# First 64 queries of every diagonal chunk: half of TensorE's columns for scores, half of its rows for values, two heads side by side

## The chip, the cores and the metric

One NeuronCore of one Trainium2 chip. The core has five engines with queues of their own, each strictly in the order written for it: TensorE (PE; its weight loads are listed separately as PEld), VectorE (DVE), ScalarE (ACT), GpSimd (POOL) and SyncE (SP, which issues DMAs). The metric is the device time of one execution in microseconds, as a median over several runs; less is better. Everything is float32.

## The reference

A transformer block on 4 batches of 512 tokens, 512 features: a layer norm, then causal attention and a mixture of experts on the same normed input, both added to the input.

```
xn  = layernorm(x)
c_Q = xn @ W_DQ.T ; c_KV = xn @ W_DKV.T                 # latents of 128
q = [c_Q @ W_UQ.T , rope(c_Q @ W_QR.T)]                 # 16 heads, 128 + 64
k = [c_KV @ W_UK.T , rope(xn @ W_KR.T)] ; v = c_KV @ W_UV.T
s = clip(q k^T, -80, 80), -inf where key > query
attn = softmax(s / sqrt(192)) @ v ; att = attn @ W_O.T
moe = shared_expert(xn) + sum over the 3 best of 7 experts, weighted
out = x + att + moe
```

The change concerns `s` and `softmax(s) @ v`. The kernel works in the latent: a head's query is folded with its key weights, so the keys of all heads are the latent `c_KV` itself (plus 64 rotary dimensions), and the values are again `c_KV`; each head's value and output weights are folded into one matrix that is applied afterwards.

## The kernel before

**Stages.** First the norm, the routing and the shared expert, then the routed experts (with the projections of attention woven in), and from about 663 us to the end attention alone. Attention is a loop over 32 pairs of heads (`pairs`: 4 batches of 8 pairs), counter `i`. All work of the loop is wrapped in `keep(...)`, so each engine's queue has the order in which the code is written.

**Layout.** `lat(b, n)` is a 128 x 512 slice of `xnT` for batch `b`: n=0 the query latent, n=1 the keys (latent on partitions, the 512 keys along the free axis), n=2 the rotary keys, twice, on partitions 0-63 for a pair's first head and on 64-127 for its second, n=3 the values (keys on partitions, in four chunks `kc` of 128). Scores are made transposed: keys on the 128 partitions, queries along the free axis. For key chunk `kc` only the queries from `kc*128` on count, so the chunks are 512, 384, 256 and 128 queries wide (`PT_W`). On the diagonal 128 x 128 block of each chunk the half above the diagonal is set to zero afterwards by a product with the triangle `tri` on GpSimd (L1445).

**One turn of the loop (L1658-1688), in TensorE's order.** `scores(i)`: eight matmuls of the latent part (L1408; heads j=0,1, chunks in the order 0, 2, 1, 3), then eight of the rotary part (L1419), where the two heads use rows 0-63 and 64-127 of the array and run side by side. Then for the next pair: `rotary_query` (L1260, output `pqr`), first `query` (L1275, `pq`); in even turns `sums` (L1508, the softmax denominators of two earlier pairs); `values(i-1, 0)` (L1489, `av`); the second `query`; `values(i-1, 1)`; in even turns from i=4 on `project_out` (L228 with tile `op`, 56 passes). A float32 matmul stands in the trace as two passes, each with a weight load of its own.

**PSUM.** Eight banks. Five have fixed names: `a0`, `a1` (chunk 0 of the two heads), `b0`, `b1` (chunks 1 and 3), `c` (chunk 2 of the first head). Three more, tag `pj`, go round: chunk 2 of the second head (`sd`), `pqr`, `pq`, `av`, `pq`, `av` take them one after the other, each waiting until the tile that had the bank has been read.

**After the scores (`weights`, L1429).** VectorE clips each bank into the SBUF tile `pt` (L1437), in the order a0, a1, sd, c, b0, b1; ScalarE takes the exponential in place (L1441), GpSimd masks. Between the third exponential and the fourth ScalarE copies `pqr` out (L1266, `qraw`); after the fifth it copies `pq`. VectorE then turns the rotary query (`rope`: L1246 and four times L1249; in odd turns right after the clips, in even turns after the reciprocal L1510 of the sums). GpSimd adds up the weights of a pair (`su`, L1469 and L1473). In odd turns VectorE ends with `divide` (L1540, L1546, L1549: four products and four sums over 128 x 512).

**Queues.** DMAs of the loop are SyncE's (`m`, `rb`) and GpSimd's (three row gathers `yg`, L1635, in even turns).

Of the kernel before, what the change touches and what calls it, by code (L numbers as in the profile page):

```python
# [12 lines left out]
I32 = mybir.dt.int32  # L13
# [23 lines left out]
QK_SCALE = 1.0 / math.sqrt(DH + DHR)  # L37

PT_W = [S - kc * P for kc in range(TPB)]


@with_exitstack
def kernel(
# [52 lines left out]
    for j in range(4):  # L96
# [11 lines left out]

    pos_i = const.tile([P, NTT, TOPK], I32, tag="pos_i", name="pos_i")
    wk = const.tile([P, NTT, TOPK], F32, tag="wk", name="wk")  # L110

    idx_i = const.tile([P, 4, NBLK], I32, tag="idx_i", name="idx_i")
    es_i = const.tile([P, NUNIT], I32, tag="es_i", name="es_i")

    used_i = const.tile([P, 1], I32, tag="used_i", name="used_i")
# [9 lines left out]
        [wb.tile([P, 2, D // 2], F32, tag=f"f{i}_{k}", name=f"f{i}_{k}") for k in range(3)]  # L125
        for i in range(3)
    ]

    half = [slice(0, S // 2), slice(S // 2, S)]

# [1062 lines left out]
    def project(b, psum):  # L1193

        if b % 2 == 0:
            two = psum(f"pj_kr_{b}")
            for c in range(DC):
                for j in range(2):
                    r = slice(j * DHR, (j + 1) * DHR)
                    keep(  # L1200
                        nc.tensor.matmul(
                            two[r, :],
                            krT[:, c, r],
                            xnT[:, c, ts(b + j, S)],
                            start=(c == 0),
                            stop=(c == DC - 1),
                        )
                    )
            raw = hw.tile([P, S], F32, tag="raw", name=f"kraw_{b}")
            keep(nc.scalar.copy(raw, two))  # L1210
            turned[b] = hw.tile([P, S], F32, tag="kr", name=f"kr_{b}", bufs=1)
            rope(turned[b], raw, f"k{b}")
        ps = []
        for wT, name in ((dqT, "cq"), (dkvT, "ckv")):
            p = psum(f"pj_{name}_{b}")
            for c in range(DC):
                keep(
                    nc.tensor.matmul(
                        p, wT[:, c, :], xnT[:, c, ts(b, S)], start=(c == 0), stop=(c == DC - 1)
                    )  # L1220
                )
            ps.append(p)
        keep(nc.scalar.copy(lat(b, 0), ps[0]))
        keep(nc.vector.tensor_copy(lat(b, 1), ps[1]))

        src = turned[b - b % 2][(b % 2) * DHR : (b % 2 + 1) * DHR, :]
        for j in range(2):
            keep(nc.vector.tensor_copy(lat(b, 2)[j * DHR : (j + 1) * DHR, :], src))

    turned = {}  # L1230

    def turn_keys(b, psum=None):
        if psum is None:
# [86 lines left out]
    def attention_steps(s):  # L1320

        for k in loads.get(s, []):
            loaded[k] = pieces[k][0]()
        for k in firsts.get(s, []):
            steps.extend(pieces[k][1](loaded[k]))
        if s == late + 2:
            dst, src = (lat(0, i).rearrange("p (k f) -> p k f", k=TPB) for i in (3, 1))
            steps.extend(turn4(dst, src))

    QUARTER = {0: 0, 4: 1, 7: 2, 10: 3}  # L1330
    POPS = (3, 2, 2, 2, 3, 3, 3, 3, 3, 3, 2, 1, 0, 0, 0, 0, 2, 2, 0, 0, 2)
# [45 lines left out]
    ap = ctx.enter_context(tc.tile_pool(name="ap", bufs=2))  # L1377
    mw = ctx.enter_context(tc.tile_pool(name="mw", bufs=1))
    ps_s = ctx.enter_context(tc.tile_pool(name="ps_s", bufs=1, space=PSUM))
    ps_p = ctx.enter_context(tc.tile_pool(name="ps_p", bufs=3, space=PSUM))  # L1380

    def psum(name):
# [7 lines left out]
    def scores(i):  # L1390
        b = pairs[i][0]
        qr, *qc = qs.pop(i)
        bank = {}
        for j in range(2):
            bank[j, 0] = ps_s.tile([P, S], F32, tag=f"a{j}", name=f"sa_{i}_{j}")
            bank[j, 1] = bank[j, 3] = ps_s.tile([P, S], F32, tag=f"b{j}", name=f"sb_{i}_{j}")
        bank[0, 2] = ps_s.tile([P, S], F32, tag="c", name=f"sc_{i}")
        bank[1, 2] = psum(f"sd_{i}")

        def where(j, kc):  # L1400
            o = 3 * P if kc == 3 else 0
            return bank[j, kc][:, o : o + PT_W[kc]]

        order = [(j, kc) for kc in (0, 2, 1, 3) for j in range(2)]
        for j, kc in order:

            keep(
                nc.tensor.matmul(  # L1408
                    where(j, kc),
                    lat(b, 1)[:, ts(kc, P)],  # L1410
                    qc[j][:, kc * P :],
                    start=(kc != 3),
                    stop=False,
                )
            )
        for j, kc in order:
            r = slice(j * DHR, (j + 1) * DHR)
            keep(
                nc.tensor.matmul(  # L1419
                    where(j, kc),  # L1420
                    lat(b, 2)[r, ts(kc, P)],
                    qr[r, kc * P :],
                    start=False,
                    stop=(kc != 1),
                )
            )
        return bank

    def weights(i, bank, then, behind):  # L1429

        pt = ap.tile([P, 5 * S], F32, tag="pt", name=f"pt_{i}")

        def clip(to, src):
            keep(nc.vector.tensor_scalar(to, src, CLIP, -CLIP, ALU.min, ALU.max))  # L1437

        def exp(t):

            keep(nc.scalar.activation(t, t, AF.Exp, scale=QK_SCALE))  # L1441

        def mask(t, at, k=1, step=P):
            m = t[:, at : at + P]
            keep(nc.gpsimd.tensor_mul(m, m, tri))  # L1445

        for j in range(2):
            a = pt[:, ts(j, S)]
            clip(a, bank[j, 0])
            exp(a)  # L1450
            mask(pt, PT[j, 0])
        half = 2 * P
        for j in (1, 0):
            clip(pt[:, PT[j, 2] : PT[j, 2] + half], bank[j, 2][:, :half])
        exp(pt[:, ts(2, S)])
        for j in range(2):
            mask(pt, PT[j, 2])
        then()
        for j in range(2):
            t = pt[:, ts(3 + j, S)]  # L1460
            clip(t, bank[j, 1])
            exp(t)
            mask(pt, PT[j, 1])
            mask(pt, PT[j, 3])
        behind()
        su = []
        for j in range(2):
            t = ap.tile([P, S], F32, tag="su", name=f"su_{i}_{j}", bufs=4)
            keep(nc.gpsimd.tensor_copy(t[:, :P], pt[:, PT[j, 0] : PT[j, 0] + P]))  # L1469
            for kc in range(1, TPB):  # L1470
                prev = pt[:, PT[j, 0] + P : PT[j, 0] + S] if kc == 1 else t[:, kc * P :]
                keep(
                    nc.gpsimd.tensor_add(  # L1473
                        t[:, kc * P :], prev, pt[:, PT[j, kc] : PT[j, kc] + PT_W[kc]]
                    )
                )
            su.append(t)
        pts[i], sus[i] = pt, su

    og = {}  # L1480

    def values(i, j):

        b, q = pairs[i][0], i // 2
        pt = pts[i]
        av = psum(f"av_{i}_{j}")
        for kc in range(TPB):
            keep(
                nc.tensor.matmul(  # L1489
                    av[:, kc * P :],  # L1490
                    lat(b, 3)[:, ts(kc, P)],
                    pt[:, PT[j, kc] : PT[j, kc] + PT_W[kc]],
                    start=(kc == 0),
                    stop=(kc == TPB - 1),
                )
            )
        if q not in og:
            og[q] = ap.tile([P, 4, S], F32, tag="og", name=f"og_{q}")
        keep(nc.scalar.copy(og[q][:, 2 * (i % 2) + j, :], av))
# [158 lines left out]
    for i in range(n):  # L1658
        more = i + 1 < n
        even = i % 2 == 0  # L1660
        q = i // 2 - 1
        held = scores(i)
        raw_copy, turn_q = rotary_query(i + 1, psum(f"pqr_{i + 1}")) if more else (nothing, nothing)
        qc_copy = query(i + 1, 0, psum(f"pq_{i + 1}_0")) if more else nothing
        weights(i, held, raw_copy, nothing if even else turn_q)
        qc_copy()
        if even and i > 0:
            spread_by_dma(q, sums(q))
        if even:
            turn_q()  # L1670
        if i > 0:
            values(i - 1, 0)
        if more:
            query(i + 1, 1, psum(f"pq_{i + 1}_1"))()
        if i < 2:
            project(2 + i, psum)
        if 1 < i < 5:
            turn_keys((2, 3, 1)[i - 2], psum)
        if i > 0:
            values(i - 1, 1)  # L1680
        if even and i > 2:
            project_out(q - 1, first_added=lambda: combine(q))
        if i == 1:
            combine(0)
        if even and i != 2 or i == 1:
            fetch((i + 1) // 2)
        if not even and i > 1:
            divide(q)
# [2 lines left out]

    def last_heads():
        combine(NTT - 1)
        values(n - 1, 0)
        values(n - 1, 1)
        last_rc.append(sums(q))
# [54 lines left out]
```

## Time and profile before

| | |
|---|---|
| time, median of 10 runs | 1348.55 us (1348.04 to 1349.01) |
| the profiled execution | 1349.36 us, its span 1347.6 us |
| TensorE busy | 1329.9 us, 99% of the span |
| VectorE / GpSimd / ScalarE busy | 975.5 / 853.1 / 398.8 us |
| granted TensorE clock | 0.999 |
| latent scores L1408, 512 passes | 512-, 384-, 256- and 128-wide, all with 128 x 128 weights |
| values L1489, 512 passes | the same four widths |
| an odd turn and an even turn (i = 11 and 12) | 13.76 and 27.51 us from scores to scores |

How to read it: TensorE's busy time is close to the span, but its rows overlap (the recorded end of a pass lies after the start of the next one), so what a pass costs is read from start to start, not from its duration. A row of the timeline has a start in microseconds, a length, the engine, the line, the operation with its operands (for TensorE `weights columns*rows` and the moving tile's shape), how many instructions were merged into it, and in brackets what it waited for. The page's digits for the last half of the span show GpSimd at eight or nine tenths, VectorE at seven or eight.

### The profile page before, as it was taken

To read this page: it belongs to the slowest core of one execution; us is meant where nothing else is said; L and a number is where in the kernel's file an instruction comes from. 1 tells how busy PE (TensorE), PEld (TensorE's weight loads), DVE (VectorE), ACT (ScalarE), POOL (GpSimd) and SP (SyncE) were. 2 spreads that over 40 slices of the span, in tenths; PEclk is the share of its full clock that TensorE was granted. 3 is DMA by queue.
4 is the path that set the end of the run, shared out by engine and by line. 5 is a ranking of instruction groups with operands and counts; after the bars stand their busy time and mean duration, and the time that the engine had idled before them with its cause. 6 is when DMAs were issued, how large, how long until landed. Compare 5 with 4: busy or idle time off the path is not lost.

```text
span 1347.6 us, 17895 instructions
## 1 busy us (share of the span) xinstructions
PE 1329.9 (99%) x5949; PEld 992.6 (74%) x5949; DVE 975.5 (72%) x1422; ACT 398.8 (30%) x694; POOL 853.1 (63%) x956
## 2 busy tenths in 40 slices
PE   9999999999999999999999999999999999999997
PEld 8777888888888888877655666666666676666675
DVE  7679576676766677676468679877788777798774
ACT  3331223222323322212223323323333323233231
POOL 5112675554545565523177788888898888888883
PEclk9999999999999999999999999999999999999999
DMA  7850255666667675523401331243322333313332
GB/s 280 193 153 17 74 148 161 191 195 184 186 167 205 172 223 159 159 84 98 141 24 53 109 110 35 86 131 110 109 64 66 121 110 110 94 48 117 102 120 76
DMA packets 174101, 167.90 MB, mean 125 GB/s; under 512 B 57904, under 2 KB 136752, under 8 KB 174000
## 3 DMA queue, kind: packets, MB, share of 16 engines
q1 hardware_dynamic: 161264, 133.10, 33.3%
q0 software_dynamic: 12736, 33.57, 8.0%
q8 instruction: 49, 0.80, 0.2%
q14 instruction: 52, 0.43, 0.1%
HBM read 116.02 MB, written 34.87 MB: 112 GB/s over the span
## 4 chain that ended last, share of the span: by engine, by line
PE 93%; DVE 5%; DMA 1%; issue 1%; ACT 0%; SPq 0%; POOL 0%; DVEq 0%; ACTq 0%; POOLq 0%
PE op L228 14%; PE hr L228 11%; PE av L1489 10%; PE yr L228 10%; PE gr L228 9%; PE sb L1408 4%; PE sa L1408 4%; PE pq L1275 4%; PE sa L1419 3%; PE pqr L1260 2%; PE sb L1419 2%; PE ys L228 2%; PE gs L228 2%; PE sb L1508 2%; PE hs L228 1%; PE h_s L142 1%
## 5 line engine op out<-in xcount | busy, mean ns | idle before, releaser
L180 POOL DMA_INDIRECT xs<-xn_d,idx_i x208 | 230.7, 1109 | 192.7 <-DVE xT L197 133.8
L1445 POOL TENSOR_TENSOR pt<-pt,tri 128x128 f32<-128x128 f32 x256 | 140.0, 568 | 67.9 <-ACT pt L1441 61.4
L1441 ACT ACTIVATE pt<-pt 128x512 f32<-128x512 f32 x160 | 94.5, 628 | 257.7 <-DVE pt L1437 256.6
L1489 PEld LDWEIGHTS av<-pt,xnT 128*128 128x128 f32 x512 | 95.4, 190 | 83.7 <-issue 47.7
L1489 PE MATMUL av<-pt,xnT 128*128 128x512 f32 (+3 forms) x512 | 149.8, 436 | 0.0
L228 PE MATMUL op<-m,og 128*128 128x256 f32 x512 | 118.7, 380 | 0.8 <-DVE og L1540 0.8
L1249 DVE TENSOR_TENSOR swap_q<-qraw,sinT 32x512 f32<-32x512 f32 x128 | 117.6, 919 | 1.7
L1473 POOL TENSOR_TENSOR su<-su,pt 128x256 f32<-128x256 f32 (+1 forms) x128 | 105.3, 822 | 10.0
L228 PEld LDWEIGHTS op<-m,og 128*128 128x128 f32 x512 | 95.9, 190 | 15.0 <-DVE og L1540 1.9
L1437 DVE TENSOR_SCALAR pt<-sa 128x512 f32<-128x512 f32 x64 | 41.1, 682 | 74.6 <-PE sa L1419 74.6
L1583 POOL TENSOR_TENSOR acc<-acc,v 128x512 f32<-128x512 f32 x64 | 85.9, 1344 | 14.3 <-DVE acc L1586 8.5
L1635 POOL DMA_INDIRECT yg<-y_d,pos_i x48 | 54.6, 1137 | 57.3 <-issue 51.3
L228 PE MATMUL op<-m,s 128*128 128x256 f32 x384 | 88.1, 379 | 0.0
L1473 POOL TENSOR_TENSOR su<-pt 128x384 f32<-128x384 f32 x64 | 83.9, 1311 | 0.0
L228 PEld LDWEIGHTS op<-m,s 128*128 128x128 f32 x384 | 73.0, 190 | 9.9
L1586 DVE TENSOR_TENSOR acc<-op,acc 128x512 f32<-128x512 f32 x48 | 31.7, 686 | 55.0 <-POOL acc L1583 47.4
L1648 DVE SCALAR_TENSOR_TENSOR acc<-yg,wk,acc 128x512 f32<-128x512 f32 x48 | 56.7, 1182 | 19.1 <-POOL acc L1583 18.0
L1579 ACT COPY v<-op 128x512 f32<-128x512 f32 x64 | 37.5, 586 | 108.4 <-PE op L228 107.2
L1540 DVE TENSOR_TENSOR og<-og,rb 128x512 f32<-128x512 f32 x64 | 68.3, 1126 | 0.6 <-PE rb L1528 0.2
L228 PE MATMUL yr<-w,at_r 128*128 128x256 f32 x288 | 67.1, 380 | 0.5 <-DVE at_r L349 0.3
L228 PE MATMUL hr<-xT,w 128*128 128x256 f32 x288 | 66.1, 379 | 0.0
L228 PE MATMUL gr<-xT,w 128*128 128x256 f32 x288 | 66.1, 379 | 0.0
(337 smaller groups left out, 2804.6 us busy)
## 6 DMA issues: line engine op xcount, KB each, us to landing
m<-m_d SPq DMA_DIRECT2D x112, 256.0 KB, 5.2
w<-in_L_ffn_W_dram SPq DMA_DIRECT2D x52, 512.0 KB, 3.9
rb<-rc SPq DMA_DIRECT2D x240, 64.0 KB, 2.0
w<-in_L_ffn_Wg_dram SPq DMA_DIRECT2D x26, 512.0 KB, 3.5
y_d<-v_yr SPq DMA_DIRECT2D x36, 256.0 KB, 2.3
y_d<-none SPq DMA_DIRECT2D x24, 256.0 KB, 4.5
acc<-in_L_attn_x_dram SPq DMA_DIRECT2D x16, 256.0 KB, 5.4
xn_d<-xp SPq DMA_DIRECT2D x16, 256.0 KB, 3.2
```

Source lines behind the costliest of these rows:

```text
L180: nc.gpsimd.indirect_dma_start(out=xs[blk][:, q, :], out_offset=None, in_=xn_d[:, :], in_offset=bass.IndirectOffsetOnAxis(ap=idx_i[:, q, b ...
L228: nc.tensor.matmul(banks[k][:, t, :], a[p][:, j, ts(t, P)], b[p][:, j, :], start=(k not in used), stop=(t == j == 1), skip_group_check=True,)
L1249: keep(nc.vector.tensor_mul(swap[there, :], raw[here, :], tables[1][here, :]))
L1408: nc.tensor.matmul(where(j, kc), lat(b, 1)[:, ts(kc, P)], qc[j][:, kc * P :], start=(kc != 3), stop=False,)
L1419: nc.tensor.matmul(where(j, kc), lat(b, 2)[r, ts(kc, P)], qr[r, kc * P :], start=False, stop=(kc != 1),)
L1441: keep(nc.scalar.activation(t, t, AF.Exp, scale=QK_SCALE))
L1445: keep(nc.gpsimd.tensor_mul(m, m, tri))
L1473: nc.gpsimd.tensor_add(t[:, kc * P :], prev, pt[:, PT[j, kc] : PT[j, kc] + PT_W[kc]])
L1489: nc.tensor.matmul(av[:, kc * P :], lat(b, 3)[:, ts(kc, P)], pt[:, PT[j, kc] : PT[j, kc] + PT_W[kc]], start=(kc == 0), stop=(kc == TPB - 1),)
L1540: keep(nc.vector.tensor_mul(o[:, j, :], o[:, j, :], rb))
L1583: keep(nc.gpsimd.tensor_add(block, block, v))
L1648: nc.vector.scalar_tensor_tensor(acc[:, g, :], yg, wk[:, g, k : k + 1], acc[:, g, :], ALU.mult, ALU.add)
```

## The change

For the first 64 queries of a diagonal block only the chunk's first 64 keys count. The change treats these 64 x 64 corners apart.

- **Scores.** The latent matmuls leave out each chunk's first 64 queries (widths 448, 320, 192, 64). A second loop makes them with 64 columns of weights, i.e. the chunk's first 64 keys: the first head on array columns 0-63, the second on 64-127, in PSUM partitions to match. For this the second head's keys stand with the two halves of each chunk swapped: a new pair of tiles per batch, `second_head(b)` (two ScalarE copies of 128 x 256 for the keys, two VectorE copies of 64 x 512 for the values), and swapped rotary keys in `lat(b, 2)`. The rotary matmuls keep their widths.
- **Values.** `values_edge(i)`: for each chunk and head a matmul with 64 rows (the chunk's first 64 keys: partitions 0-63 for the first head, 64-127 for the second), 128 columns of weights and 64 queries. Its 8 matmuls for the pair before stand right behind the rotary scores in TensorE's order, ahead of `rotary_query`. `values` keeps its place with the widths 448, 320, 192, 64.
- **PSUM.** Both `av` banks are now taken in `values_edge`. `pqr` and the second `pq` therefore take bank `a1` instead of a `pj` bank.
- **The rest.** A second triangle with swapped halves, `tri_s`, for the second head's masks; the tile `idx_i` moves to the pool `wb`; at the end `values_edge(31)` stands before the last two `values`.

```diff
+HP = P // 2
@@ -1224,10 +1226,32 @@
         keep(nc.vector.tensor_copy(lat(b, 1), ps[1]))
         src = turned[b - b % 2][(b % 2) * DHR : (b % 2 + 1) * DHR, :]
-        for j in range(2):
-            keep(nc.vector.tensor_copy(lat(b, 2)[j * DHR : (j + 1) * DHR, :], src))
+        keep(nc.vector.tensor_copy(lat(b, 2)[:DHR, :], src))
+        for h in range(2):
+            to, of = (halves(t, k) for t, k in ((lat(b, 2)[DHR:, :], h), (src, 1 - h)))
+            keep(nc.vector.tensor_copy(to, of))
     turned = {}
+    def halves(t, h):
+        return t.rearrange("p (k h f) -> p k h f", k=TPB, h=2)[:, :, h]
+    def second_head(b):
+        both = [hw.tile([P, S], F32, tag=t, name=f"{t}_{b}") for t in ("ckv_s", "ckvt_s")]
+        for h in range(2):
+            keep(nc.scalar.copy(halves(both[0], h), halves(lat(b, 1), 1 - h)))
+            keep(nc.vector.tensor_copy(both[1][ts(h, HP), :], lat(b, 3)[ts(1 - h, HP), :]))
+        swapped[b] = both
+    swapped = {}
+    def keys(b, j):
+        return swapped[b] if j else (lat(b, 1), lat(b, 3))
     def turn_keys(b, psum=None):
         if psum is None:
@@ -1326,6 +1350,7 @@
         if s == late + 2:
             dst, src = (lat(0, i).rearrange("p (k f) -> p k f", k=TPB) for i in (3, 1))
             steps.extend(turn4(dst, src))
+            steps.append(lambda: second_head(0))
     QUARTER = {0: 0, 4: 1, 7: 2, 10: 3}
     POPS = (3, 2, 2, 2, 3, 3, 3, 3, 3, 3, 2, 1, 0, 0, 0, 0, 2, 2, 0, 0, 2)
@@ -1377,6 +1402,10 @@
     ap = ctx.enter_context(tc.tile_pool(name="ap", bufs=2))
     mw = ctx.enter_context(tc.tile_pool(name="mw", bufs=1))
     ps_s = ctx.enter_context(tc.tile_pool(name="ps_s", bufs=1, space=PSUM))
+    tris = [tri, mw.tile([P, P], F32, tag="tri_s", name="tri_s")]
+    for j in range(2):
+        keep(nc.gpsimd.tensor_copy(tris[1][ts(j, HP), :], tri[ts(1 - j, HP), :]))
     ps_p = ctx.enter_context(tc.tile_pool(name="ps_p", bufs=3, space=PSUM))
     def psum(name):
@@ -1406,11 +1435,25 @@
             keep(
                 nc.tensor.matmul(
-                    where(j, kc),
-                    lat(b, 1)[:, ts(kc, P)],
-                    qc[j][:, kc * P :],
+                    where(j, kc)[:, HP:],
+                    keys(b, j)[0][:, ts(kc, P)],
+                    qc[j][:, kc * P + HP :],
                     start=(kc != 3),
                     stop=False,
+                    skip_group_check=True,
+                )
+            )
+        for j, kc in order:
+            keep(
+                nc.tensor.matmul(
+                    where(j, kc)[ts(j, HP), :HP],
+                    lat(b, 1)[:, kc * P : kc * P + HP],
+                    qc[j][:, kc * P : kc * P + HP],
+                    start=False,
+                    stop=False,
+                    skip_group_check=True,
                 )
             )
         for j, kc in order:
@@ -1422,6 +1465,7 @@
                     qr[r, kc * P :],
                     start=False,
                     stop=(kc != 1),
+                    skip_group_check=True,
                 )
             )
         return bank
@@ -1440,28 +1484,28 @@
             keep(nc.scalar.activation(t, t, AF.Exp, scale=QK_SCALE))
-        def mask(t, at, k=1, step=P):
-            m = t[:, at : at + P]
-            keep(nc.gpsimd.tensor_mul(m, m, tri))
+        def mask(j, kc):
+            m = pt[:, PT[j, kc] : PT[j, kc] + P]
+            keep(nc.gpsimd.tensor_mul(m, m, tris[j]))
         for j in range(2):
             a = pt[:, ts(j, S)]
             clip(a, bank[j, 0])
             exp(a)
-            mask(pt, PT[j, 0])
+            mask(j, 0)
         half = 2 * P
         for j in (1, 0):
             clip(pt[:, PT[j, 2] : PT[j, 2] + half], bank[j, 2][:, :half])
         exp(pt[:, ts(2, S)])
         for j in range(2):
-            mask(pt, PT[j, 2])
+            mask(j, 2)
         then()
         for j in range(2):
             t = pt[:, ts(3 + j, S)]
             clip(t, bank[j, 1])
             exp(t)
-            mask(pt, PT[j, 1])
-            mask(pt, PT[j, 3])
+            mask(j, 1)
+            mask(j, 3)
         behind()
         su = []
         for j in range(2):
@@ -1479,19 +1523,42 @@
     og = {}
+    av_of = {}
+    def values_edge(i):
+        b, pt = pairs[i][0], pts[i]
+        av = av_of[i] = [psum(f"av_{i}_{j}") for j in range(2)]
+        for kc in range(TPB):
+            for j in range(2):
+                r, at = ts(j, HP), PT[j, kc]
+                keep(
+                    nc.tensor.matmul(
+                        av[j][:, kc * P : kc * P + HP],
+                        keys(b, j)[1][r, ts(kc, P)],
+                        pt[r, at : at + HP],
+                        start=(kc == 0),
+                        stop=False,
+                        skip_group_check=True,
+                    )
+                )
     def values(i, j):
         b, q = pairs[i][0], i // 2
-        pt = pts[i]
-        av = psum(f"av_{i}_{j}")
+        pt, av = pts[i], av_of[i][j]
         for kc in range(TPB):
+            at = PT[j, kc]
             keep(
                 nc.tensor.matmul(
-                    av[:, kc * P :],
-                    lat(b, 3)[:, ts(kc, P)],
-                    pt[:, PT[j, kc] : PT[j, kc] + PT_W[kc]],
-                    start=(kc == 0),
+                    av[:, kc * P + HP :],
+                    keys(b, j)[1][:, ts(kc, P)],
+                    pt[:, at + HP : at + PT_W[kc]],
+                    start=False,
                     stop=(kc == TPB - 1),
+                    skip_group_check=True,
                 )
             )
         if q not in og:
@@ -1660,7 +1727,11 @@
         even = i % 2 == 0
         q = i // 2 - 1
         held = scores(i)
-        raw_copy, turn_q = rotary_query(i + 1, psum(f"pqr_{i + 1}")) if more else (nothing, nothing)
+        if i > 0:
+            values_edge(i - 1)
+        free = bank("a1")
+        raw_copy, turn_q = rotary_query(i + 1, free(f"pqr_{i + 1}")) if more else (nothing, nothing)
         qc_copy = query(i + 1, 0, psum(f"pq_{i + 1}_0")) if more else nothing
         weights(i, held, raw_copy, nothing if even else turn_q)
         qc_copy()
@@ -1671,11 +1742,13 @@
         if i > 0:
             values(i - 1, 0)
         if more:
-            query(i + 1, 1, psum(f"pq_{i + 1}_1"))()
+            query(i + 1, 1, free(f"pq_{i + 1}_1"))()
         if i < 2:
             project(2 + i, psum)
         if 1 < i < 5:
             turn_keys((2, 3, 1)[i - 2], psum)
+        if i % NPAIR == 5 and i // NPAIR + 1 < B:
+            second_head(i // NPAIR + 1)
         if i > 0:
             values(i - 1, 1)
         if even and i > 2:
@@ -1691,6 +1764,7 @@
     def last_heads():
         combine(NTT - 1)
+        values_edge(n - 1)
         values(n - 1, 0)
         values(n - 1, 1)
         last_rc.append(sums(q))
```

More of the change, by code (lines that the diff above doesn't have):

```diff
@@ L110 @@
     wk = const.tile([P, NTT, TOPK], F32, tag="wk", name="wk")
-    idx_i = const.tile([P, 4, NBLK], I32, tag="idx_i", name="idx_i")
     es_i = const.tile([P, NUNIT], I32, tag="es_i", name="es_i")
@@ L127 @@
     ]
+    idx_i = wb.tile([P, 4, NBLK], I32, tag="idx_i", name="idx_i")
     half = [slice(0, S // 2), slice(S // 2, S)]
```

## The prediction

> **What bounds the kernel now.** I read the page first: busy shares, and the chain that ended last.
>
> ```profile
> PE 1329.9 (99%) x5949; PEld 992.6 (74%) x5949; DVE 975.5 (72%) x1422; ACT 398.8 (30%) x694; POOL 853.1 (63%) x956
> PE 93%; DVE 5%; DMA 1%; issue 1%; ACT 0%; SPq 0%; POOL 0%; DVEq 0%; ACTq 0%; POOLq 0%
> ```
>
> TensorE is the bound, so a change pays by what it does to the starts of TensorE's passes. Next, its timeline in an odd turn, i=11.
>
> ```profile
> 884.87 1.88 PE L1408 MATMUL sa<-qc,xnT 128*128 128x512 f32 x4
> 886.59 0.59 PE L1408 MATMUL sc<-qc,xnT 128*128 128x256 f32 x2
> 887.02 0.59 PE L1408 MATMUL sd<-qc,xnT 128*128 128x256 f32 x2
> 887.45 1.90 PE L1408 MATMUL sb<-qc,xnT 128*128 128x384 f32 x8
> 889.28 1.13 PE L1419 MATMUL sa<-qr,xnT 64*128 64x512 f32 x4
> ...
> 890.67 1.03 PE L1419 MATMUL sb<-qr,xnT 64*128 64x384 f32 x8
> 891.63 1.12 PE L1260 MATMUL pqr<-xnT,qrT 128*128 128x512 f32 x2
> 892.60 1.02 PE L1275 MATMUL pq<-xnT,a_h 128*128 128x512 f32 x2
> ```
>
> Starts: four 512-wide passes take 1.72 us, two of 256 take 0.43. A pass costs 0.84 ns a column. Where the array's tiling changes there is more: the last eight latent passes take 1.83 instead of 1.72 (a drain of 0.10), and `pqr` then needs 0.97 for 0.86 of columns (its first 128-column weight load, 0.11, stands bare). The rotary rows show the two heads' passes side by side: the last eight take 0.96, which is 0.86 for four passes' columns and a drain. What a short pass costs is in the routing stage: 128x128 weights, 72 columns.
>
> ```profile
> 146.49 1.01 PE L789 MATMUL tq<-tg,row_of 128*128 128x72 f32 x8
> 147.33 0.64 PE L228 MATMUL ys<-w,at_s 128*128 128x256 f32 x2
> ```
>
> Eight passes take 0.84 us, 0.105 each (0.11 after the first), where 72 columns would take 0.06: the next weight load is the floor. Lastly VectorE from the clips of i=11 to those of i=12, and ScalarE beside it.
>
> ```profile
> 890.44 1.29 DVE L1437 TENSOR_SCALAR pt<-sa 128x512 f32<-128x512 f32 x2 [4.01 <-PE sa L1419]
> ...
> 892.30 1.28 DVE L1437 TENSOR_SCALAR pt<-sb 128x512 f32<-128x512 f32 x2
> 893.56 0.99 DVE L1246 TENSOR_TENSOR qr<-qraw,cosT 128x512 f32<-128x512 f32 x1
> ...
> 898.03 4.47 DVE L1540 TENSOR_TENSOR og<-og,rb 128x512 f32<-128x512 f32 x4
> ...
> 906.55 1.28 DVE L1437 TENSOR_SCALAR pt<-sa 128x512 f32<-128x512 f32 x2
> ```
>
> ```profile
> 892.96 0.57 ACT L1266 COPY qraw<-pqr 128x512 f32<-128x512 f32 x1
> 893.42 1.15 ACT L1441 ACTIVATE pt<-pt 128x512 f32<-128x512 f32 x2
> ```
>
> VectorE has no gap from 890.44 to 906.55: clips, rotary query, `divide`. So the clips of the even turn start 3.5 us after its rotary scores did (903.04), while those of the odd turn wait 4 us for TensorE. That lateness costs nothing now: nobody on TensorE waits for banks a0 and a1 that soon.
>
> **The change, part by part.** TensorE first; T is the start of an odd turn's rotary scores (889.28).
>
> Scores: 16 passes lose 64 columns, 0.86 us. But 64 columns are 0.054, below the 0.11 floor, in three of the four chunk-3 passes (the fourth meets the switch): 0.17 back, 0.69 saved. New are 8 side-by-side passes of 64 columns with 64-column weights. The nearest row is the rotary-key projection with the same half-column weights: it takes 0.14 over its columns for a switch, of which 0.05 is the bare load, and its second load starts 0.05 after the first, on both halves at once. So 8 x 0.057 + 0.14 = 0.60, net -0.09 a pair. If the halves' loads didn't overlap, 0.11 a pass: net +0.33. I take -0.09, since that row has the same tiling.
>
> Values: 0.86 less 4 x 0.055 for the chunk-3 passes: 0.64 saved. The corners are 8 side-by-side passes of 64 columns with 128-column weights: the 0.11 floor, 0.88, less 0.06 because the last one drains sooner; no switch, since the rotary scores have the same tiling. Net +0.18. The floor is the certain part here; at column rate it would be 0.42 less.
>
> [...]
>
> TensorE alone is thus 0.10 slower a pair, 3.2 in all, plus 0.4 for the last `values_edge`, which pays its own switches: +3.5.
>
> The wait that is added: `pqr` now goes to bank a1 and must wait until VectorE has clipped a1; before, it needed a `pj` bank long free. In an odd turn the clip of a1 ends at T+2.45, and `pqr` comes at T+2.35+0.82: no wait. In the even turn `pqr` comes at T+13.76+0.10+2.35+0.82 = T+17.03; the clip of a1 ends at 907.83, T+18.55, and 0.05 later TensorE can go (as it does behind L1540 at 1328.31): it stands for 1.57. Everything on TensorE is queued behind `pqr`: `pq`, `sums`, both `values`, `project_out`, the next scores; ScalarE's `qraw`, the exponentials behind it and the reciprocal wait for those.
>
> VectorE follows. In odd turns `pqr` starts 0.82 later, ends at T+4.30, ScalarE's copy `qraw` runs T+4.34 to T+4.91, and VectorE's L1246, at T+4.28 now, starts at T+4.95. The whole gapless block moves by 0.67, the even clip of a1 with it: the stand is 2.24.
>
> Something is given back: `sums` of even turns waits 0.47 for GpSimd's `su` today (1.47 from start to start where its passes, load and drain take 1.00; 13 times). Behind a later `pqr` it doesn't.
>
> Per two turns: 0.20 + 2.24 - 0.47 = 1.97. It applies to the even turns 4 to 30, 14 times (turn 4 has no wait for `su`, but 0.45 less of a stand): 27.6. Turn 2 follows an odd turn without `divide` and is spared; turns 0 to 3 and the end leave 1.0 of TensorE's own. After the stand, even turns have room: VectorE idles 2.9 and 2.8 us in them for GpSimd, so the reciprocal, which starts some 1.3 later than now against the clips, hides.
>
> Small work: `second_head` puts two VectorE copies of 64x512 ahead of `divide` in turns 5, 13 and 21; the same shape took 0.42 (L1228), so 3 x 0.84 = 2.5 straight into the stand. The copies for batch 0 and the split rotary keys lie in the expert stage beside TensorE's 99%, the ScalarE copies in an engine 30% busy, `tri_s` once ahead of the first mask; without that cover they would cost some 6 us together (four at 0.42, eight at the 0.57 of L1266). GpSimd has the same masks, SyncE the same DMAs in the same order; the `rb` copies, behind the later reciprocal, are wanted only by `divide` in the next odd turn, over 20 us on. `values_edge` needs the masks of the pair before: these end 7.8 us ahead in even turns, 20.9 in odd ones; no wait.
>
> Sum: 27.6 + 1.0 + 2.5 = +31. The profiled execution had 1349.36, so 1380.5; the median is 0.8 lower, so **1380 us**.
>
> A stand of 2.2 us is a thing the trace doesn't have: TensorE's longest wait, 1.8 in the routing stage, passes at granted clock 1.00. [...]
>
> **Rivals.**
> On the other side: the block shrinks. `divide` takes 8.5 us here with GpSimd busy for 8.2 of them; at the end of the kernel (1327.57 to 1332.75) the same eight operations, GpSimd idle, take 5.2. If GpSimd's sums fell elsewhere, VectorE would be 3.3 earlier, over the 2.24: no stand. Then +3.5 for TensorE, minus 13 x 0.47 = 6.1 for `su`: 1346. It decides once the block is 2.2 us shorter. Against it: masks and `su` hang on the same clips and exponentials and move along.
>
> Half a stand: contention falls by about 1.1 a block: 1380 - 15 = 1365.
>
> Loads that don't overlap, or more contention: the first costs +0.42 in each stretch from an even `pqr` to the next odd scores, 14 x 0.42 = 6; half a microsecond more in each block gives 7: 1386 to 1393.
>
> The split pays: if the 0.11 floor didn't hold with two row groups, TensorE alone would end at 1349 + 3.5 - 13 (32 x 0.42) - 6 = 1333 without the stand; with it, some 1373, since the saving in the odd turn disappears in the stand.
>
> **How the numbers follow.** Forecast 1372 to 1386: 0.62. More contention or serial loads, up to 1395: 0.16. Half a stand or cheap corners, 1358 to 1372: 0.14. No stand, 1346: 0.05, of which 0.03 is faster and 0.02 same. The split pays without a stand: 0.03, faster. The range takes the first three but their outer ends: 1362 to 1394. A measurement of this kernel tells 0.2% (2.7 us) from no change. Faster 0.05, same 0.03, slower 0.92.
>
> **What would show it.** Right: `pqr` in even turns waiting about 2.2 us for the clip L1437, none in odd turns; even to odd starts as before plus 2; corner rows of the values 0.11 apart, those of the scores 0.057; `sums` without its wait for `su`; L1246 in odd turns waiting for `qraw`. Wrong: even clips that start within 1.5 us of their rotary scores, or corner passes of the values at 0.06.

## The result

The changed kernel takes 1402.64 us (median of 8 runs, 1399.11 to 1404.40) against 1348.60 (28 runs): 1.0399 times the time before, 95% interval 1.0390 to 1.0409. The direction was forecast, the size was not: +54 us where +31 was predicted, and above the range's upper end of 1394. The profiled execution took 1402.17 us, its span 1400.1.

Busy shares and the chain that ended last, on the page of the changed kernel:

```profile
PE 1352.8 (97%) x6973; PEld 1034.6 (74%) x6973; DVE 963.4 (69%) x1434; ACT 405.9 (29%) x702; POOL 830.2 (59%) x958
PE 79%; DVE 15%; issue 3%; DMA 1%; ACT 1%; POOL 1%; DVEq 0%; SPq 0%; ACTq 0%; POOLq 0%
```

VectorE has gone from 5% to 15% of the chain: TensorE waits for it. The waits of TensorE say where (us together, times, longest):

```profile
PE pqr L1284 <- DVE pt L1481: 30.2, 14, 3.4
PE tok_ps L774 <- DVE ohs L762: 4.7, 3, 1.8
```

Fourteen waits of `pqr` for a clip (L1481 is the clip's new line), 30.2 us together: the stand, in the turns that were named. One of them in TensorE's timeline (turn 10; T is the start of the rotary scores of turn 9, 857.96):

```profile
871.85 1.13 PE L1462 MATMUL sa<-qr,xnT 64*128 64x512 f32 x4
...
874.72 0.27 PE L1538 MATMUL av<-pt,xnT 64*128 64x64 f32 x1
...
874.83 0.27 PE L1538 MATMUL av<-pt,xnT 64*128 64x64 f32 x1
...
876.99 1.58 PE L1284 MATMUL pqr<-xnT,qrT 128*128 128x512 f32 x2 [1.88 <-DVE pt L1481]
878.36 1.91 PE L1299 MATMUL pq<-xnT,a_h 128*128 128x512 f32 x2
880.21 1.40 PE L1575 MATMUL sb<-su,ones 128*32 128x512 f32 x8
881.54 2.05 PE L1555 MATMUL av<-pt,xnT 128*128 128x448 f32 x8
```

The values' corner passes are 0.11 apart. Those of the scores, one turn earlier, are 0.06 apart:

```profile
857.51 0.22 PE L1450 MATMUL sc<-qc,xnT 128*64 128x64 f32 x1
...
857.57 0.22 PE L1450 MATMUL sc<-qc,xnT 128*64 128x64 f32 x1
...
857.63 0.40 PE L1450 MATMUL sb<-qc,xnT 128*64 128x64 f32 x8
```

Behind the stand the two passes of `pqr` take 1.37 us instead of 0.97 and those of `pq` 1.85 instead of 0.95, though nothing is waited for. The stretches of these two turns with the clock that TensorE was granted (columns: stretch, its length, busy times and instruction counts by engine, clock, DMA share, GB/s):

```profile
857.96:871.85 13.89, 13.89 (x91) 9.36 (x87) 11.94 (x16) 5.67 (x10) 9.35 (x12) 1.00 0.08 29
871.85:876.99 5.14, 3.26 (x36) 2.35 (x33) 5.07 (x7) 0.56 (x2) 4.76 (x6) 1.00 0.00 0
876.99:880.93 3.94, 3.94 (x8) 1.16 (x12) 1.80 (x4) 3.43 (x7) 2.91 (x7) 0.57 0.00 0
880.93:884.35 3.42, 3.42 (x19) 1.81 (x12) 2.59 (x1) 0.61 (x2) 3.04 (x7) 1.00 0.00 0
```

After the stand the clock is 0.57 for 3.9 us, then full again. The trace's clock records have 13 such stretches at half speed in the attention stage, eleven of 3.41 us and two of 6.83; the kernel before has none (left out here and below is the one at the end of a trace, in these two 3.0 and 3.3 us after TensorE's last pass). This is the part that the sum had put at nothing. VectorE between the clips of turns 9 and 10:

```profile
859.12 1.29 DVE L1481 TENSOR_SCALAR pt<-sa 128x512 f32<-128x512 f32 x2 [4.54 <-PE sa L1462]
...
862.94 0.69 DVE L1270 TENSOR_TENSOR qr<-qraw,cosT 128x512 f32<-128x512 f32 x1 [0.67 <-ACT qraw L1290]
...
875.66 1.28 DVE L1481 TENSOR_SCALAR pt<-sa 128x512 f32<-128x512 f32 x2
```

The forecast wait for `qraw` is there, 0.67 us, to T+4.98.

Four of the runs below (e1 to e4) were on a chip where every kernel, the one before too (1378.69 us), needs about 30 us more, and their attention begins at 692 to 699 us instead of 662 to 663; so the comparisons use the attention stage alone, from the first latent scores to the end of a profile. It is 684.39 us in the kernel before, 684.40 in a second profile of it, and 737.69 in the changed kernel: +53.3. The view of the kernel before:

```profile
663.19:1347.58 684.39, 676.88 (x2814) 440.63 (x2814) 520.04 (x598) 218.37 (x388) 553.58 (x656) 1.00 0.30 92
```

### The profile page after: what moved, and what is told of

Its sections match the earlier page's. It is cut to its first block, busy times and chain, and to the rows that moved or that the text cites. A ratio compares the mean times of both kernels' runs of the same rounds, so it can differ in the third digit from the quotient of the medians.

```text
span 1400.1 us, 19989 instructions
## 1 busy us (share of the span) xinstructions
PE 1352.8 (97%) x6973; PEld 1034.6 (74%) x6973; DVE 963.4 (69%) x1434; ACT 405.9 (29%) x702; POOL 830.2 (59%) x958
## 4 chain that ended last, share of the span: by engine, by line
PE 79%; DVE 15%; issue 3%; DMA 1%; ACT 1%; POOL 1%; DVEq 0%; SPq 0%; ACTq 0%; POOLq 0%
PE op L230 14%; PE hr L230 10%; PE yr L230 10%; PE gr L230 10%; PE av L1555 5%; DVE og L1607 4%; PE pq L1299 3%; PE pqr L1284 3%; PE sa L1437 2%; PE sb L1437 2%; PE ys L230 2%; DVE s L1616 2%; PE gs L230 2%; PE sb L1575 1%; PE sa L1462 1%
## 5 line engine op out<-in xcount | busy, mean ns | idle before, releaser
L1489 POOL TENSOR_TENSOR pt<-pt,tri 128x128 f32<-128x128 f32 x128 | 65.5, 522 | 112.1 <-ACT pt L1485 111.7
L1273 DVE TENSOR_TENSOR swap_q<-qraw,sinT 32x512 f32<-32x512 f32 x128 | 108.8, 850 | 1.7
L1481 DVE TENSOR_SCALAR pt<-sa 128x512 f32<-128x512 f32 x64 | 41.1, 682 | 81.5 <-PE sa L1462 81.5
L1577 DVE RECIPROCAL rc<-sb 128x512 f32<-128x512 f32 x16 | 53.7, 3357 | 43.9 <-PE sb L1575 43.9
L1517 POOL TENSOR_TENSOR su<-pt 128x384 f32<-128x384 f32 x64 | 78.2, 1222 | 0.1
L1299 PE MATMUL pq<-xnT,a_h 128*128 128x512 f32 x128 | 78.2, 699 | 0.0
L1555 PEld LDWEIGHTS av<-pt,xnT 128*128 128x128 f32 x256 | 45.5, 190 | 41.7 <-issue 36.5
L1489 POOL TENSOR_TENSOR pt<-pt,tri_s 128x128 f32<-128x128 f32 x128 | 72.8, 579 | 2.6
L1274 POOL TENSOR_TENSOR qr<-qr,swap_q 128x512 f32<-128x512 f32 x32 | 45.9, 1435 | 43.1 <-DVE swap_q L1273 43.1
L1284 PE MATMUL pqr<-xnT,qrT 128*128 128x512 f32 x62 | 41.9, 764 | 30.3 <-DVE pt L1481 30.2
L1555 PEld LDWEIGHTS av<-pt,ckvt_s 128*128 128x128 f32 x256 | 46.5, 190 | 29.9 <-issue 24.8
```

Source lines behind the costliest of these rows:

```text
L1273: keep(nc.vector.tensor_mul(swap[there, :], raw[here, :], tables[1][here, :]))
L1284: keep(nc.tensor.matmul(ps, qrT[:, hp, :], lat(b, 0), start=True, stop=True))
L1299: keep(nc.tensor.matmul(ps, a_h[:, 2 * hp + j, :], lat(b, 0), start=True, stop=True))
L1489: keep(nc.gpsimd.tensor_mul(m, m, tris[j]))
L1517: nc.gpsimd.tensor_add(t[:, kc * P :], prev, pt[:, PT[j, kc] : PT[j, kc] + PT_W[kc]])
L1555: nc.tensor.matmul(av[:, kc * P + HP :], keys(b, j)[1][:, ts(kc, P)], pt[:, at + HP : at + PT_W[kc]], start=False, stop=(kc == TPB - 1), s ...
```

## The experiments

The theory after the result: TensorE stands (is idle) until bank a1 is free, and most stands (13 of 14 in the changed kernel) are followed by half the granted clock, for 3.41 us or, twice, 6.83. The rival: the short corner passes and their tiling switches make the loss, and a half-used array lowers the clock. All times are of the attention stage unless said otherwise; "per two turns" is from one odd turn's rotary scores to the next odd turn's, less the 41.27 us of the kernel before.

**The bank alone (e1).** The kernel before, no corners.

```diff
+        free = bank("a1")
-        ... rotary_query(i + 1, psum(f"pqr_{i + 1}"))
+        ... rotary_query(i + 1, free(f"pqr_{i + 1}"))
-            query(i + 1, 1, psum(f"pq_{i + 1}_1"))()
+            query(i + 1, 1, free(f"pq_{i + 1}_1"))()
```

> The kernel before, with only the bank change: the rotary query and the second query of the next pair go to bank a1, no corners, no swapped keys. Stand theory (TensorE stands for the clip of a1 in even turns, and the clock gate answers each stand with a window at half speed): in even turns pqr comes at T+16.11 and the clip ends at T+18.55, so it stands 2.5 us, in odd ones 0.15; less 0.47 for the sums, that is 2.1 to 2.2 per two turns, 14 times, 30 us; with 12 to 14 half-speed windows at about 1.65 us each another 21: 1400 us (1390 to 1408), granted clock 0.98. Corner theory (the short passes and tiling switches themselves make the loss and lower the clock): nothing of them is here, so 1349 to 1355 us, clock 0.999.

Measured 727.92 us, +43.5, and 1.0293 (1.0254 to 1.0332) times the time before. TensorE's waits in that stage:

```profile
PE pqr L1260 <- DVE pt L1437: 31.2, 14, 2.3
```

Two turns take 2.01 more where the clock held and 3.65 where it didn't. It fell 9 times, not 12 to 14 (granted clock 0.98 over the stage), so the total is at the lower end of the stand theory's range (41 to 59 us over before), and far above the 0 to 6 of the rival. A change of two bank names, with not one corner, costs four fifths of the whole loss.

**The stand filled (e2), and half filled (e8).** In the changed kernel, behind `values_edge`, matmuls of a zero tile that are added into the first `av` bank: two in e2, one in e8.

```diff
+        for _ in range(2 if even and i > 3 else 0):
+            keep(nc.tensor.matmul(av_of[i - 1][0], zero, lat(pairs[i][0], 0),
+                                  start=False, stop=False, skip_group_check=True))
```

> The changed kernel, with two matmuls of a zero tile (512 columns, 1.83 us) added into the first av bank behind values_edge in the even turns from 4 on: the result stays, TensorE is busy while it would stand. Stand theory with the clock as its second half: VectorE and the start of pqr stay as they are, but no half-speed window follows: 1402.6 less 23, 1379 us (1374 to 1385), clock 0.999. If the clock falls because of the corners' half-used array, or the fall is harmless: 1400 or more, clock 0.98.

e2 measured 714.64 us, 23.05 less than the changed kernel, with more work on TensorE: the extra matmuls make it faster. (Against the kernel before it is 1.0220, 1.0179 to 1.0260, times the time.) No half-speed stretch is left in the stage:

```profile
699.13:1413.78 714.65, 702.36 (x3894) 487.45 (x3894) 515.34 (x606) 222.32 (x394) 541.39 (x659) 1.00 0.29 88
```

beside the same view of the changed kernel:

```profile
662.40:1400.09 737.69, 699.55 (x3838) 482.17 (x3838) 506.39 (x606) 224.88 (x394) 529.48 (x658) 0.96 0.28 85
```

> The changed kernel with one zero matmul (0.97 us) in each stand instead of two; about 0.9 us of the stand stays idle, 2.4 in turns 6, 14 and 22. If the gate answers to idle above about half of a 3.4 us window: no half-speed window but perhaps in those three turns, attention stage 714.6 to 719. If any idle of a microsecond is enough: 730 or more.

e8 measured 720.36 us (1384.32 in all, 1.0262, 1.0244 to 1.0281, times the time before). Its `pqr` still waits 14 times:

```profile
PE pqr L1284 <- DVE pt L1483: 15.4, 14, 2.3
```

So the fill in it is too short to set when `pqr` starts; and its undisturbed even turns are 1.58 longer than before, those of e2 1.59. So e2's fill hides in the stand too. The clock fell in turns 6, 14 and 22 alone, where 2.3 us stay idle. It ends 1.4 above the range given because these three falls cost 6.0 us together: 2.9 in turn 6, where the half speed lasts 6.83 us, and 1.65 and 1.44 in the others. The other eleven waits of e8, about 0.8 us each, and the three of e2, at most 1.4 us, were not followed by half speed.

**The stand taken away (e4).** VectorE's block is cut by leaving out the four products of `divide` (the division of the outputs by the softmax sums) in all but the last two pairs.

```diff
         for j, rb in enumerate(spread.pop(q)):
-            keep(nc.vector.tensor_mul(o[:, j, :], o[:, j, :], rb))
+            if q == n // 2 - 1:
+                keep(nc.vector.tensor_mul(o[:, j, :], o[:, j, :], rb))
```

> The changed kernel without the four products of divide, except for the last two pairs (left out: the division of the outputs by the softmax sums). VectorE's gapless block is 4.5 us shorter, more than the stand. Stand theory: pqr waits in no turn, sums no longer waits for su, the clock stays: 1348.6 + 3.5 - 6.1 = 1346 us (1344 to 1352), clock 0.999. Corner theory: TensorE's queue is unchanged, so 1395 or more, clock 0.98.

Measured 683.26 us, 1.1 below before, and 0.9991 (0.9960 to 1.0022) of its time. No wait of `pqr` is left and the clock is 1.00:

```profile
692.40:1375.66 683.26, 675.32 (x3838) 477.91 (x3838) 455.60 (x546) 223.56 (x394) 516.55 (x658) 1.00 0.30 92
```

TensorE's queue is that of the changed kernel, instruction by instruction. Odd turns are 0.12 longer than before, even turns 0.35 shorter: the corners' own passes cost less than the 0.47 that `sums` gives back. The corner theory falls here. (VectorE has less to do in e4 than in the kernel before, so this is no measure of the corners at equal work.)

These runs split the loss: e4 less before is -1.1 (TensorE's own work and the wait for `su`), e2 less e4 is 31.4 (the stands), changed less e2 is 23.05 (the clock). The sum is 53.3.

**The corners one by one.** The scores' corners alone (e3): `values` at full width on the swapped keys, `pqr` and `pq` back in the round banks.

```diff
-        pt, av = pts[i], av_of[i][j]
+        pt, av = pts[i], psum(f"av_{i}_{j}")
...
-                    pt[:, at + HP : at + PT_W[kc]],
-                    start=False,
+                    pt[:, at : at + PT_W[kc]],
+                    start=(kc == 0),
...
-        if i > 0:
-            values_edge(i - 1)
-        free = bank("a1")
```

> The scores' corners alone: swapped keys and masks as in the changed kernel, values at their full widths, banks as in the kernel before. By the prediction's sum TensorE saves 0.09 a pair and nobody waits: 1348.6 - 2.9 = 1345.7 us (1343.5 to 1348), clock 0.999. If the loads of the two column halves do not overlap: +0.33 a pair, 1359. Corner theory: slower, 1355 or more.

Measured 685.98 us: +1.6 instead of -2.9; in all 1.000 (0.9975 to 1.0024). In odd turns the corners do what the sum said: they are 0.08 shorter. But even turns are as long as before, and in turns 6, 14 and 22 `sums` stands for a clip, 4.4 us together:

```profile
PE sb L1574 <- DVE pt L1481: 4.4, 3, 1.5
```

That is `second_head`: the second of its two VectorE copies took 1.40 us, not 0.42, beside a busy GpSimd.

All corners, the values' ones later (e6): `values_edge(i - 1)` directly ahead of `values(i - 1, 0)`, its second bank `a1`, the queries in the round banks.

```diff
-        av = av_of[i] = [psum(f"av_{i}_{j}") for j in range(2)]
+        av = av_of[i] = [psum(f"av_{i}_0"), bank("a1")(f"av_{i}_1")]
...
         if i > 0:
+            values_edge(i - 1)
             values(i - 1, 0)
```

> All corners, but those of the values stand ahead of values(i-1, 0) instead of behind the scores, with their second bank a1 (free by then) and the queries back in the round banks. Stand theory: no wait for a1, clock 1.00; the values' corners pay tiling switches of their own, 0.21 in even and 0.42 in odd turns: +0.31 and +0.52 a turn against before, 13, plus 1.6 for the next scores' wait for a1 in odd turns and 4.4 for sums behind second_head: attention stage 703 us (698 to 707). Corner theory: the same short passes and more switches, so 738 or more, with half-speed windows.

Measured 696.41 us, +12.0 and 1.0084 (1.0066 to 1.0103): no stand of `pqr`, no half speed (granted clock 0.998 in the whole execution), and the values' corners with switches of their own cost 0.65 in odd turns, in even ones 0.15 is gained since `sums` no longer waits. The sum was 6.6 too dear: it had left out the 0.47 that `sums` gives back in even turns (6.1 in 13 turns), the wait for a1 (1.6) didn't come, and `sums` stood 2.2, not 4.4; against that, the values' corners cost 0.13 more in odd turns than it said.

The version that came out ahead (e5b): the scores' corners alone, in chunks 0 to 2, with `second_head` a turn later.

```diff
-        if i % NPAIR == 5 and i // NPAIR + 1 < B:
+        if i % NPAIR == 6 and i // NPAIR + 1 < B:
...
-        for j, kc in order:
+        for j, kc in order[:-2]:
...
-                    where(j, kc)[:, HP:],
+                    where(j, kc)[:, HP * (kc < 3) :],
```

> The kernel before, unchanged, for one more profile beside the others. Both theories: 684.4 us from the first scores to the end, as in the first profile, clock 1.00 there, whatever the expert stage ahead of it takes on this chip.

> Only the scores' corners, only in chunks 0 to 2 (chunk 3 stays 128 wide), with second_head's copies one turn later, in an even turn where VectorE has idle time. By the sum: leaving chunk 3 whole gives back 0.057 x 2 of corners for 0.054 saved, so -0.15 a pair, -4.8 in all, and no turn in which sums stands for a late clip: attention stage 679.6 us (678 to 682), clock 1.00, in all 0.36% faster than before where nothing disturbs the expert stage. Corner theory: 688 or more.

The kernel before gave 684.40 again. e5b measured 681.85 and 1345.74 us in all, 0.9976 (0.9966 to 0.9986) of the time before: faster than both kernels, by half of what was expected. Odd turns are 0.14 shorter, as worked out; even turns are exactly as long as before, though their scores too are 0.14 shorter. What takes it back sits between an odd turn's scores and the even turn's `values`: counted from the rotary scores of turn 9, `pqr` of turn 10 starts 0.14 earlier than before (15.98 against 16.12), but GpSimd's last `su` ends at 18.45 (18.47) and `values` starts at 19.48 (19.50).

**Moving `sums` (e11, e12).** Was it the wait for GpSimd's `su`?

```diff
-        if even and i > 0:
-            spread_by_dma(q, sums(q))
-        if even:
-            turn_q()
         if i > 0:
             values(i - 1, 0)
+        if even and i > 0:
+            spread_by_dma(q, sums(q))
+        if even:
+            turn_q()
```

> The scores' corners in chunks 0 to 2 (as in e5b_best), and sums of the even turns behind values(i-1, 0) instead of ahead of it. In e5b_best the odd turns got the 0.14 us of the sum and the even turns nothing; the reading is that sums there waits for GpSimd's su, which hangs on the odd turn's scores and takes back what TensorE saves. If so, sums 1.9 us later in the queue waits for nobody: even turns shorter by 0.14 + 0.47, thirteen times 0.6, 8 us under e5b_best: attention stage 674 us (672 to 677), in all 1338 us. If what took the gain back in even turns is another wait (the reciprocal's chain on VectorE, the add of acc): 680 to 682, or slower, since the reciprocal starts later.

> The kernel before with sums alone moved behind values(i-1, 0). By the same reading the wait of 0.47 in 13 even turns goes: 684.4 - 6.1 = 678.3 us of attention (677 to 680), 1342.5 us in all. If another wait stands there: 683 to 685.

A miss, in both: 692.15 and 694.49 us, 1.0049 (1.0035 to 1.0063) and 1.0078 (1.0062 to 1.0093) times the time before. The wait for `su` is gone, and `values` now waits in its place, for the clip that frees its bank; in e12:

```profile
PE av L1489 <- DVE pt L1437: 11.1, 14, 0.8
```

That wait alone is nearly twice the 6.1 us that the move was to save. So in the kernel before TensorE already met VectorE's late block in even turns (in turn 10 the clip ends at 18.88, 0.62 ahead of `values`): `sums` had been the work that covered it. What TensorE saves between an odd turn's scores and that point is lost at it, which fits e5b's even turns.

## Why the prediction was right and wrong

The failed step is the clock. The sum had the stands' own time and nothing for the clock, in the number and in the range. Measured: 23.05 us (changed kernel less e2), in 13 of the 14 stands. The trace of before could not show it, since its longest idle was 1.8 us, at full clock; the prediction noted that a stand of 2.2 us is not in that trace, but carried no price for it, which came out nearly as large as the rest, into the upper end. With it the sum would have been 1403. That this comes so close is partly luck: without the clock the loss is 30.3 us (e2 less before) against the sum's 31, but some of its terms were too dear and others too cheap.

Step by step, for two turns from turn 7 on:

| term | predicted | measured |
|---|---|---|
| TensorE's own work | +0.20 | +0.24 (2 x 0.12) |
| the stand | +2.24 | +1.94 (e2 less e4) |
| `sums` no longer waits for `su` | -0.47 | -0.47 |
| the clock | 0 | +1.64 (2.59 where it lasted 6.83 us) |
| `second_head`, each of three times | +0.84 | +1.50 |

- The corners: right in the sum. Values' corner passes are 0.111 apart (0.11 predicted), scores' 0.058 (0.057), net -0.08 for the scores (-0.09). 64 moving columns take 0.111 with 128 columns of weights and 0.058 with 64, which fits the weight load as the floor. Even so the scores' corners gain by running side by side: two heads' passes take 0.058 together for columns that take 0.108 one after the other, 1.9 times the rate. The tiling switch (0.15) and the chunk-3 passes left at 64 columns (0.17) take most of it back. The values' corners, at 0.111, don't.
- The stand: right in place, count and cause, 0.3 too large. VectorE's block moved by the 0.67 that was worked out, but its first operation behind the wait then took 0.69 us instead of 0.99: in the later place GpSimd is busy for 0.12 us of it, before for 0.86.
- `second_head`: its copies were priced by rows (0.42) that had little or no GpSimd work beside them; here the second copy lies beside GpSimd's `qr` and `su` and takes 1.40.
- Rivals: the shrinking block is what e4 made by hand, and it ended where that rival did, at no loss; contention in the kernel itself hardly changed (`divide` takes 8.52 us with GpSimd busy for 8.17 of them, in turn 9 here as in turn 11 before). Loads that don't overlap, and a split that pays: neither.

## What to carry to other kernels

Reusing a bank moves a wait to whoever reads it: ask in which turn the reader is late, not whether it has idle time on average. When a change makes TensorE stand for some two microseconds where it never did, carry the clock's price into the range, since it can come near the wait (here 23.05 us beside 31.4); and if the stand can't be removed, matmuls of zeros into a bank that is open anyway take the clock's part back (23 us here). Before splitting a matmul into corners, look for the shortest pass that the trace has with the same weights: here, with 128 float32 columns of weights, passes of 64 and of 72 moving columns cost 0.11 us, what 128 columns cost at 0.84 ns each.

## What the runs showed of the hardware

Waits of `pqr` in the attention stage, and what the granted clock did there:

| run | waits | together, longest (us) | half-speed stretches | granted clock |
|---|---|---|---|---|
| kernel before | none | | none | 1.00 |
| changed kernel | 14 | 30.2, 3.4 | 13 | 0.96 |
| e1 | 14 | 31.2, 2.3 | 9 | 0.98 |
| e8 | 14 | 15.4, 2.3 | 3 | 0.99 |
| e2 | 3 | 4.3, 1.4 | none | 1.00 |
| e4 | none | | none | 1.00 |

In the changed kernel turn 4's wait, 1.48 us, was followed by no half speed. Ten waits of 1.86 to 1.88 us were followed by 3.41 us of it each, and the three of 3.34 or 3.35 us (turns 6, 14 and 22, behind `second_head`) by 3.41, 6.83 and 6.83 (the last two begin 1.4 to 1.5 us before the wait ends). In the kernel before, TensorE's longest wait, 1.78 us in the routing stage, passed at full clock.

The length of a wait alone doesn't tell what follows: the waits of e1 are 2.23 us on average, longer than those ten, and five of the fourteen passed at full clock. No run varies one thing alone between such waits, so what decides was not shown. But every wait of 1.86 us and more in the changed kernel was followed by half speed, and nine of the fourteen in e1: a stand of some 2 us was not safe here, and a fall cost 1.44 to 1.65 us (2.59 to 2.9 where it lasted 6.83).
